# Two layers of attention over 16 images: scores with j on partitions, two heads on halves of the array, a constant softmax shift

## The chip, the cores and the metric

One core of a Trainium2 chip runs the whole program in one launch. The metric is the device time of one execution in microseconds; the median of the runs counts. All data are float32 in HBM at the start and at the end.

## The reference

x has 16 images (b) of 256 channels and 32 x 32 positions. Two layers are applied, each `x = x + attention(groupnorm(x))`:

```
gn: for each image and each pair of neighbouring columns h (16 groups):
    subtract the mean over channels, w and the pair; divide by sqrt(var + 1e-5)
q, k, v = Wq.g + bq, Wk.g + bk, Wv.g + bv          (256 x 256 weights, 1024 positions)
4 heads of d = 64:
    s[i, j]   = q_i . k_j + rel_i . q_j             rel[d, i] = rel_h[d, y] + rel_w[d, w]
    attn[i,:] = softmax over j of s[i, :]
    out[d, i] = sum over j of attn[i, j] * v[d, j]
```

For each image, layer and head the scores are 1024 x 1024.

## The kernel before

A unit is one layer of one image; there are 32, ordered so that layer 0 of the next image alternates with layer 1 of the one before. A unit has 8 blocks: 4 heads times two halves of 512 rows i. x of up to three images stays in SBUF (two tiles of 128 channels side by side) and is updated in place.

For a unit, `norm_slices` sums x over columns on VectorE, averages across partitions by a matmul with a constant matrix (`pm`), and subtracts, squares and scales on GpSimd. `v_slices` makes v with positions on partitions. `kq_slices` makes, for each head, one tile with k on partitions 0-63 and q on 64-127; VectorE then copies q to the upper half of `qrel`, whose lower half holds rel. So one matmul over 128 partitions gives both terms of the scores: [q_i; rel_i] . [k_j; q_j].

`scores` (L232) treats 128 rows i at a time: two matmuls of 128 x 128 weights with 512 columns fill two banks of PSUM (L240), VectorE takes the negative row maximum (L248), ScalarE the exponential with that maximum as bias and the row sum (L251), VectorE the reciprocal (L255) and the scaling of the row (L256). `transposes` (L261) turns the block's four tiles, 128 columns j at a time, by four TensorE transposes into a bank of PSUM (L266), and ScalarE or VectorE copies it to SBUF (L271, L273). `attend` (L278) multiplies with v: the weights are v of two heads (128 columns), and the rows of one head are used (L284). `finish` (L292) adds the result and v's bias to x; attn is normalized already.

The order of each engine's queue is the order in which the code emits the work. The loop at the end emits, for each block and each 128 rows, the scores of the current block, then two transposes and two products of the block before, then one slice of the next unit's norm or projections (from the second block of a unit on). Where two units in a row are of the same layer, `kq_slices` of the second come at once at its start. Loads and stores are issued from SP's queue. PSUM holds two tiles of two banks (scores, projections), two of one bank (transposes, means) and two for the output.

Of the kernel before, what the change touches and what calls it, by code (L numbers as in the profile page):

```python
# [9 lines left out]
F32 = mybir.dt.float32  # L10
AF = mybir.ActivationFunctionType
ALU = mybir.AluOpType
AX = mybir.AxisListType


@with_exitstack
def kernel(
# [17 lines left out]
    P = 128  # L35
    B, C, W, H = x.shape
    N = W * H
    NL = len(layers)
    HEADS = layers[0]["rel_h"].shape[1]
    D = C // HEADS  # L40
    CC = C // P
    NT = N // P
    HALF = 512
    NH = N // HALF
    G = 16
    GT = H // G
    COUNT = C * W * GT
    EPS = 1e-5
    IPB = HALF // P
    BPU = HEADS * NH  # L50
    assert (D, CC, NT, NH, NL) == (64, 2, 8, 2, 2)

    const = ctx.enter_context(tc.tile_pool(name="const", bufs=1))
# [3 lines left out]
    bpool = ctx.enter_context(tc.tile_pool(name="bpool", bufs=6))  # L57
    vpool = ctx.enter_context(tc.tile_pool(name="vpool", bufs=2))
    ppool = ctx.enter_context(tc.tile_pool(name="ppool", bufs=10))
    stat = ctx.enter_context(tc.tile_pool(name="stat", bufs=6))  # L60
    ptpool = ctx.enter_context(tc.tile_pool(name="ptpool", bufs=4))
    ps_s = ctx.enter_context(tc.tile_pool(name="ps_s", bufs=2, space=bass.MemoryType.PSUM))
    ps_t = ctx.enter_context(tc.tile_pool(name="ps_t", bufs=2, space=bass.MemoryType.PSUM))
    ps_o = ctx.enter_context(tc.tile_pool(name="ps_o", bufs=2, space=bass.MemoryType.PSUM))

# [1 line left out]
    xt = {}  # L67

    def load_x(b):
        xt[b] = xpool.tile([P, CC, N], F32, tag="x", name=f"x_{b}")  # L70
        for cc in range(CC):
            nc.sync.dma_start(
                xt[b][:, cc, :], x[b, cc * P : (cc + 1) * P].rearrange("p w h -> p (w h)")
            )

    load_x(0)

# [1 line left out]
    ident = const.tile([P, P], F32, tag="ident", name="ident")  # L79
    make_identity(nc, ident)  # L80
    avg = const.tile([P, P], F32, tag="avg", name="avg")
    nc.vector.memset(avg, 1.0 / COUNT)
    mhalf = const.tile([P, H], F32, tag="mhalf", name="mhalf")
    nc.vector.memset(mhalf, -0.5)

    wkq, wv, bkq, bv, qrel = [], [], [], [], []
    for li, lw in enumerate(layers):
        wkq_l = const.tile([P, CC, HEADS, P], F32, tag=f"wkq{li}", name=f"wkq{li}")
        wv_l = const.tile([P, CC, C], F32, tag=f"wv{li}", name=f"wv{li}")
# [45 lines left out]
    for b in range(1, B):  # L135
        units += [(b, 0), (b - 1, 1)]
# [139 lines left out]
    outs = {}  # L276
# [102 lines left out]
```

## Time and profile before

| | us |
|---|---|
| median of 3 runs | 5371.05 (5367.75, 5371.05, 5399.57) |
| span of the profiled execution | 5370.3 |
| TensorE (PE) busy | 5209.0 |
| VectorE (DVE) busy | 3353.1 |
| ScalarE (ACT) busy | 2041.9 |
| GpSimd (POOL) busy | 589.5 |
| HBM, mean over the span | 7 GB/s |

The time of the profiled execution is known by its span alone, from the first to the last instruction: 5370.3 us, 0.8 us under the median. "PE" rows are matmul instructions, "PEld" rows the loads of their weights, which may overlap matmuls; a matmul's row reaches from its start to its modelled end, so rows in a row overlap. "Idle before" is the time for which the engine had nothing to run ahead of these instructions, with what ended it.

### The profile page before, as it was taken

The numbers are of one execution on the slowest core, as the hardware profiler recorded it, in microseconds if no ns is written. First come the engines' busy times: TensorE is split into PE (matmuls) and PEld (weight loads), VectorE is DVE, ScalarE is ACT, GpSimd is POOL, SyncE is SP. The second block draws the span as 40 slices with busy tenths as digits, with TensorE's granted clock in tenths as the row PEclk, the third lists the DMA queues.
The fourth block names the chain that finished last, engine by engine and source line by source line (L and its number), as shares of the span: only waits on it lengthen the run. The fifth ranks groups of instructions, "written<-read, shape, count | busy, mean of one in ns | idle before, by whom it ended". The sixth has DMA issues, their size and how long they took to land.

```text
span 5370.3 us, 46932 instructions
## 1 busy us (share of the span) xinstructions
PE 5209.0 (97%) x18712; PEld 2788.6 (52%) x18712; DVE 3353.1 (62%) x4694; ACT 2041.9 (38%) x3265; POOL 589.5 (11%) x134
## 2 busy tenths in 40 slices
PE   6999999999999999999999999999999999999999
PEld 3555555555555555555555555555555555555555
DVE  4666666666666666666666666666666666666666
ACT  2333333333333333333333333333333333333333
POOL 2001110011100111101111001110011100111000
PEclk9999999999999999999999999999999999999999
DMA  1000000000000000000000000000000000000000
GB/s 36 1 1 4 12 0 16 1 5 12 0 16 1 5 12 1 16 1 4 12 1 16 0 5 12 0 16 1 5 12 1 16 0 5 12 4 4 1 8 8
DMA packets 13787, 38.28 MB, mean 7 GB/s; under 512 B 3840, under 2 KB 5376, under 8 KB 13568
## 3 DMA queue, kind: packets, MB, share of 16 engines
q1 hardware_dynamic: 13568, 35.27, 1.8%
q8 instruction: 148, 2.42, 0.2%
q14 instruction: 71, 0.58, 0.0%
HBM read 18.49 MB, written 16.78 MB: 7 GB/s over the span
## 4 chain that ended last, share of the span: by engine, by line
PE 88%; POOL 5%; DVE 5%; ACT 1%; issue 0%; DMA 0%; SPq 0%; POOLq 0%
PE po L284 31%; PE ps L240 30%; PE pt L266 15%; PE pk L214 8%; PE pv L198 4%; POOL xc L172 3%; POOL sq L174 2%; DVE nmax L248 2%; ACT p L251 1%; DVE red_v L145 1%; DVE p L256 1%; DVE at L273 0%; PE pm_v L154 0%; DVE rden L255 0%; DMA wn<-in_L_conv_Wk_dram 0%
## 5 line engine op out<-in xcount | busy, mean ns | idle before, releaser
L284 PE MATMUL po<-at,v 128*128 128x512 f32 x4096 | 2116.0, 603 | 120.2 <-DVE at L273 120.0
L240 PE MATMUL ps<-kq,qrel 128*128 128x512 f32 x4096 | 1986.9, 599 | 1.0 <-ACT p L251 0.9
L248 DVE TENSOR_REDUCE nmax<-ps 128x1 f32<-128x1024 f32 x1024 | 1252.2, 1223 | 756.3 <-PE ps L240 754.7
L266 PEld LDWEIGHTS pt<-ident,p 128*128 128x128 f32 x8192 | 1020.9, 142 | 960.4 <-issue 779.6
L271 ACT COPY at<-pt 128x512 f32<-128x512 f32 x1024 | 600.5, 586 | 2277.9 <-PE pt L266 2277.8
L251 ACT ACTIVATE p<-ps,nmax 128x1024 f32<-128x1024 f32 x1024 | 1141.2, 1114 | 349.5 <-DVE nmax L248 349.4
L266 PE MATMUL pt<-ident,p 128*128 128x128 f32 x8192 | 1200.7, 275 | 0.3 <-DVE p L256 0.2
L240 PEld LDWEIGHTS ps<-kq,qrel 128*128 128x128 f32 x4096 | 764.0, 192 | 836.6 <-issue 823.2
L273 DVE COPY at<-pt 128x512 f32<-128x512 f32 x1024 | 705.2, 689 | 377.4 <-PE pt L266 377.3
L284 PEld LDWEIGHTS po<-at,v 128*128 128x128 f32 x4096 | 635.1, 191 | 428.7 <-DVE at L273 314.4
L256 DVE TENSOR_SCALAR p<-p,rden 128x1024 f32<-128x1024 f32 x1024 | 828.8, 809 | 34.8
L172 POOL TENSOR_TENSOR xc<-x,mean 128x2048 f32<-128x2048 f32 x32 | 144.8, 4526 | 4070.5 <-DVE mean L170 4070.5
L214 PE MATMUL pk<-xc,wkq 128*128 128x512 f32 x1024 | 463.6, 592 | 0.0
L225 DVE COPY qrel<-kq 64x1024 f32<-64x1024 f32 x128 | 88.3, 690 | 461.0 <-ACT kq L222 461.0
L214 PEld LDWEIGHTS pk<-xc,wkq 128*128 128x128 f32 x1024 | 192.3, 190 | 230.6 <-issue 216.7
L222 ACT ACTIVATE kq<-pk,bkq 128x1024 f32<-128x1024 f32 x128 | 142.6, 1114 | 445.4 <-PE pk L214 445.4
L255 DVE RECIPROCAL rden<-den 128x1 f32<-128x1 f32 x1024 | 167.0, 163 | 205.6 <-ACT p L251 153.2
L198 PE MATMUL pv<-wv,xc 128*128 128x256 f32 x1024 | 239.5, 383 | 10.7 <-POOL xc L184 10.7
L198 PEld LDWEIGHTS pv<-wv,xc 128*128 128x128 f32 x1024 | 194.2, 192 | 62.9 <-issue 22.2
L183 POOL TENSOR_TENSOR rstd<-var,mhalf 128x32 f32<-128x32 f32 x32 | 173.7, 5429 | 443.0 <-DVE rden L255 277.8
L298 DVE SCALAR_TENSOR_TENSOR x<-po,bv,x 64x512 f32<-64x512 f32 x256 | 191.7, 749 | 41.7 <-PE po L284 41.6
L251 ACT ACTIVATION_READ_ACCUMULATOR p<-ps,nmax 128x1 f32 x1024 | 197.5, 193 | 0.0
(25 smaller groups left out, 602.5 us busy)
## 6 DMA issues: line engine op xcount, KB each, us to landing
x<-in_x_dram SPq DMA_DIRECT2D x32, 512.0 KB, 4.2
out_dram<-x SPq DMA_DIRECT2D x32, 512.0 KB, 2.6
wn<-in_L_conv_Wk_dram SPq DMA_DIRECT2D x2, 256.0 KB, 3.7
wn<-in_L_conv_Wq_dram SPq DMA_DIRECT2D x2, 256.0 KB, 4.2
wn<-in_L_conv_Wv_dram SPq DMA_DIRECT2D x2, 256.0 KB, 4.5
rh<-in_L_conv_rel_h_dram SPq DMA_DIRECT2D x2, 32.0 KB, 3.3
rw<-in_L_conv_rel_w_dram SPq DMA_DIRECT2D x2, 32.0 KB, 2.8
bkq<-in_L_conv_bk_dram SPq DMA_DIRECT2D x2, 1.0 KB, 4.1
```

Source lines behind the costliest of these rows:

```text
L172: nc.gpsimd.tensor_tensor(rows(xc), rows(src), per_column(mean), ALU.subtract)
L198: nc.tensor.matmul(pv[:, i, :], xns[u][:, cc, t * P : (t + 1) * P], wv[l][:, cc, :], start=(cc == 0), stop=(cc == CC - 1),)
L214: nc.tensor.matmul(pk[:, nh, :], wkq[l][:, cc, h, :], xns[u][:, cc, nh * HALF : (nh + 1) * HALF], start=(cc == 0), stop=(cc == CC - 1),)
L240: nc.tensor.matmul(ps[:, nh, :], qrel[l][:, h, i0 : i0 + P], kqs[u, h][:, nh * HALF : (nh + 1) * HALF], start=True, stop=True,)
L248: nc.vector.tensor_reduce(nmax, ps, AX.XY, ALU.max, negate=True)
L251: nc.scalar.activation(p.rearrange("p (a n) -> p a n", a=NH), ps, AF.Exp, bias=nmax, accum_out=den)
L256: nc.vector.tensor_scalar(p, p, rden, None, ALU.mult)
L266: nc.tensor.transpose(pt[:, s * P : (s + 1) * P], probs[blk, s][:, j * P : (j + 1) * P], ident)
L271: nc.scalar.copy(t, pt)
L273: nc.vector.tensor_copy(t, pt)
L284: nc.tensor.matmul(outs[blk], vts[u][:, j, c0 : c0 + P], attnT.pop((blk, j)), start=(j == 0), stop=(j == NT - 1),)
L298: nc.vector.scalar_tensor_tensor(xs, outs.pop(blk)[r0 : r0 + D, :], bv[l][r0 : r0 + D, cc : cc + 1], xs, ALU.add, ALU.add)
```

## The change

The kernel gets two paths. `fast_path` is always run; `general_path`, a loop over images that works much as the old kernel does with a row maximum, follows it behind a branch. It is run if any softmax denominator of the fast path lies outside 1e-22 to 1e24.

In `fast_path` a block is a pair of heads (`pr`) and 512 rows i, 4 blocks a unit, and a step (blk, j) treats 128 positions j, 8 steps a block. k and q of two heads lie in one tile each, head 0 on partitions 0-63 and head 1 on 64-127, so that each score matmul has 64 rows of weights. The scores come with j on partitions and i along the columns. The term with rel is made in two parts: `positions` multiplies q with rel_h and rel_w (64 values for each j instead of 1024), and splits the result in two float32r tiles, `hi` and `lo`; in `scores` these are multiplied with `pick`, a constant matrix of zeros and ones that spreads the 64 values to the columns i. The exponential has the constant 36 subtracted in place of the maximum. Its result is the moving operand of the product with v directly; each head's result goes to its own 64 partitions of one bank. VectorE adds up the eight exponential tiles of a block; a matmul with ones sums them over partitions; the denominators go by DMA from one partition to 64 (8 on each), are inverted there, written to HBM, and read back spread to all partitions; `finish` multiplies with them. `den_all` keeps them for the test at the end.

The loop emits for each step its scores, after each odd step the products with v of two earlier steps, at the fourth step of a block the denominators of the block before and at its last step that block's `finish`, and then a slice of the next unit's preparation (from the unit's second block on). `norm_slices` has five empty slices where it had three, and two after each sum where it had one. PSUM holds three tiles of two banks (scores, projections, sums) and two for the output. The weights are loaded ahead of x, by `load_weights`, with 14 transfers a layer. `project` is as before, with two heads' k (or q) in one product; `values` is as before.

```diff
+def fast_path(ctx, tc, sh, x, out, W, den_all):
...
+    LAG = 2
...
+    ppool = ctx.enter_context(tc.tile_pool(name="ppool", bufs=8))
...
+    ps_s = ctx.enter_context(tc.tile_pool(name="ps_s", bufs=3, space=bass.MemoryType.PSUM))
+    ps_o = ctx.enter_context(tc.tile_pool(name="ps_o", bufs=2, space=bass.MemoryType.PSUM))
...
+    def positions(u, pr):
+
+        l = units[u][1]
+        pa = psum2(f"pa_{u}_{pr}")
+        for nh in range(NH):
+            nc.tensor.matmul(
+                pa[:, nh, :],
+                W.rel[l][:, pr, :],
+                qs[u, pr][:, nh * HALF : (nh + 1) * HALF],
+                start=True,
+                stop=True,
+            )
+        hi = kqpool.tile([P, N], F32R, tag="hi", name=f"hi_{u}_{pr}")
+        lo = kqpool.tile([P, N], F32R, tag="lo", name=f"lo_{u}_{pr}")
+        nc.scalar.copy(hi.rearrange("p (a n) -> p a n", a=NH), pa)
+        nc.vector.tensor_tensor(
+            lo.rearrange("p (a n) -> p a n", a=NH),
+            pa,
+            hi.bitcast(F32).rearrange("p (a n) -> p a n", a=NH),
+            ALU.subtract,
+        )
+        abh[u, pr], abl[u, pr] = hi, lo
...
+    def scores(blk, j):
+        u, pr, half = blk
+        ps = psum2(f"ps_{u}_{pr}_{half}_{j}")
+        jc = slice(j * P, (j + 1) * P)
+        ic = slice(half * HALF, (half + 1) * HALF)
+        hs = [slice(0, D), slice(D, P)]
+        for h in range(2):
+            nc.tensor.matmul(
+                ps[:, h, :], ks[u, pr][hs[h], jc], qs[u, pr][hs[h], ic], start=True, stop=False
+            )
+        for part, last in ((abh, False), (abl, True)):
+            for h in range(2):
+                nc.tensor.matmul(
+                    ps[:, h, :], part[u, pr][hs[h], jc], W.pick[hs[h], ic], start=False, stop=last
+                )
+        p = ppool.tile([P, 2, HALF], F32, tag="p", name=f"p_{u}_{pr}_{half}_{j}")
+        nc.scalar.activation(p, ps, AF.Exp, bias=W.shift)
+        probs[blk, j] = p
+        if j == 1:
+            accs[blk] = apool.tile([P, 2, HALF], F32, tag="acc", name=f"acc_{u}_{pr}_{half}")
+            nc.vector.tensor_tensor(accs[blk], probs[blk, 0], p, ALU.add)
+        elif j > 1:
+            nc.vector.tensor_tensor(accs[blk], accs[blk], p, ALU.add)
+
+    def attend(blk, j):
+        u, pr, half = blk
+        if j == 0:
+            outs[blk] = ps_o.tile([P, HALF], F32, tag="o", name=f"po_{u}_{pr}_{half}")
+        p = probs.pop((blk, j))
+        for h in range(2):
+            c0 = pr * P + h * D
+            nc.tensor.matmul(
+                outs[blk][h * D : (h + 1) * D, :],
+                vts[u][:, j, c0 : c0 + D],
+                p[:, h, :],
+                start=(j == 0),
+                stop=(j == NT - 1),
+            )
...
+    def denominators(blk):
...
+        pd = psum2(f"pd_{name}")
+        acc = accs.pop(blk)
+        for h in range(2):
+            nc.tensor.matmul(
+                pd[h * D : (h + 1) * D, 0, :], W.ones[:, :D], acc[:, h, :], start=True, stop=True
+            )
+        den = fpool.tile([P, HALF], F32, tag="den", name=f"den_{name}")
+        nc.scalar.copy(den, pd[:, 0, :])
+        for h in range(2):
+            nc.sync.dma_start(den_all[h * D : (h + 1) * D, n, :], den[h * D : h * D + 1, :])
+        r8 = fpool.tile([P, 8], F32, tag="r8", name=f"r8_{name}")
+        nc.vector.reciprocal(r8, den_all[:, n, :])
+        rd = dpool.tile([2, HALF], F32, tag="rd", name=f"rd_{name}")
+        nc.sync.dma_start(rd.rearrange("h (a b) -> (h a) b", b=8), r8)
+        rden = fpool.tile([P, HALF], F32, tag="rden", name=f"rden_{name}")
+        nc.sync.dma_start(rden, rd.unsqueeze(1).to_broadcast([2, D, HALF]))
+        return rden
...
+    def finish(blk):
...
+        nc.vector.tensor_tensor(o, outs.pop(blk), rdens.pop(blk), ALU.mult)
+        nc.vector.scalar_tensor_tensor(xs, o, W.bv[l][:, pr : pr + 1], xs, ALU.add, ALU.add)
...
+    for g in range(len(steps) + LAG):
+        if g < len(steps):
+            scores(*steps[g])
+        if g % 2 == 1:
+            for a in (g - LAG - 1, g - LAG):
+                if 0 <= a < len(steps):
+                    attend(*steps[a])
+
+        n, c = divmod(g, NT)
+        if c == LAG + 1 and n > 0:
+            rdens[blocks[n - 1]] = denominators(blocks[n - 1])
+        if c == NT - 1 and n > 0:
+            finish(blocks[n - 1])
...
+                if u + 1 < len(units):
+                    prep = chain(norm_slices(u + 1), projection_slices(u + 1))
+            next(prep, None)
...
+    fast_path(tc, sh, x, out, W, den_all)
...
+        nc.vector.tensor_scalar(low, flatden, DEN_LO, None, ALU.is_ge)
...
+        nc.vector.scalar_tensor_tensor(good, flatden, DEN_HI, low, ALU.is_le, ALU.mult)
...
+    ok = nc.values_load(flag[0:1, 0:1], min_val=0, max_val=P)
+    with tc.If(ok < P):
+        general_path(tc, sh, x, layers, out, W)
```

## Rows read from the trace of the kernel before

**Rows 1.** The page's head, busy time by engine, and the granted TensorE clock.

```profile
span 5370.3 us, 46932 instructions
PE 5209.0 (97%) x18712; PEld 2788.6 (52%) x18712; DVE 3353.1 (62%) x4694; ACT 2041.9 (38%) x3265; POOL 589.5 (11%) x134
PEclk9999999999999999999999999999999999999999
```

**Rows 2.** The page's chain that ended last, by engine and line.

```profile
PE po L284 31%; PE ps L240 30%; PE pt L266 15%; PE pk L214 8%; PE pv L198 4%; POOL xc L172 3%; POOL sq L174 2%; DVE nmax L248 2%; ACT p L251 1%; DVE red_v L145 1%; DVE p L256 1%; DVE at L273 0%; PE pm_v L154 0%; DVE rden L255 0%; DMA wn<-in_L_conv_Wk_dram 0%
```

**Rows 3.** Groups by form, TensorE matmuls: count, busy us, mean ns, idle before.

```profile
L284 PE MATMUL po<-at,v 128*128 128x512 f32 x4096 | 2116.0, 603 | 120.2 <-DVE at L273 120.0 <-ACT at L271 0.2
L240 PE MATMUL ps<-kq,qrel 128*128 128x512 f32 x4096 | 1986.9, 599 | 1.0 <-ACT p L251 0.9
...
L266 PE MATMUL pt<-ident,p 128*128 128x128 f32 x8192 | 1200.7, 275 | 0.3 <-DVE p L256 0.2
...
L214 PE MATMUL pk<-xc,wkq 128*128 128x512 f32 x1024 | 463.6, 592 | 0.0
L198 PE MATMUL pv<-wv,xc 128*128 128x256 f32 x1024 | 239.5, 383 | 10.7 <-POOL xc L184 10.7
...
L154 PE MATMUL pm_v<-red_v,avg 128*128 128x16 f32 x128 | 17.1, 246 | 12.0 <-DVE red_v L145 12.0
```

**Rows 4.** The chain in order of time, projections: start us, us, what.

```profile
214.51 13.73 PE pk L214 x32
```

**Rows 5.** Timeline, TensorE, two stretches: start, us, engine, line, operation, idle before.

```profile
2000.64 1.88 PE L240 MATMUL ps<-kq,qrel 128*128 128x512 f32 x4
2000.65 0.19 PEld L240 LDWEIGHTS ps<-kq,qrel 128*128 128x128 f32 x1 [0.24 <-issue]
...
2001.08 0.19 PEld L240 LDWEIGHTS ps<-kq,qrel 128*128 128x128 f32 x1 [0.24 <-issue]
...
2002.36 0.60 PE L266 MATMUL pt<-ident,p 128*128 128x128 f32 x4
...
5356.07 0.30 PEld L284 LDWEIGHTS po<-at,v 128*128 128x128 f32 x2 [0.48 <-ACT at L271]
```

**Rows 6.** Groups by form, ScalarE and VectorE.

```profile
L251 ACT ACTIVATE p<-ps,nmax 128x1024 f32<-128x1024 f32 x1024 | 1141.2, 1114 | 349.5 <-DVE nmax L248 349.4
...
L271 ACT COPY at<-pt 128x512 f32<-128x512 f32 x1024 | 600.5, 586 | 2277.9 <-PE pt L266 2277.8
...
L298 DVE SCALAR_TENSOR_TENSOR x<-po,bv,x 64x512 f32<-64x512 f32 x256 | 191.7, 749 | 41.7 <-PE po L284 41.6
...
L255 DVE RECIPROCAL rden<-den 128x1 f32<-128x1 f32 x1024 | 167.0, 163 | 205.6 <-ACT p L251 153.2
...
L222 ACT ACTIVATE kq<-pk,bkq 128x1024 f32<-128x1024 f32 x128 | 142.6, 1114 | 445.4 <-PE pk L214 445.4
...
L145 DVE TENSOR_REDUCE red_v<-sq 128x16 f32<-128x1024 f32 x64 | 77.7, 1215 | 116.5 <-POOL sq L174 116.5
...
L205 ACT COPY v<-pv 128x1024 f32<-128x1024 f32 x64 | 64.8, 1012 | 248.1 <-PE pv L198 248.1
...
L119 DVE TENSOR_TENSOR qrel<-rh,rw 64x1024 f32<-64x1024 f32 x8 | 9.5, 1221 | 0.1
```

**Rows 7.** Groups by form, GpSimd.

```profile
L183 POOL TENSOR_TENSOR rstd<-var,mhalf 128x32 f32<-128x32 f32 x32 | 173.7, 5429 | 443.0 <-DVE rden L255 277.8 <-DVE var L179 165.2
L172 POOL TENSOR_TENSOR xc<-x,mean 128x2048 f32<-128x2048 f32 x32 | 144.8, 4526 | 4070.5 <-DVE mean L170 4070.5
```

**Rows 8.** DMA issues by line: count, KB each, median us from issue to landing.

```profile
bkq<-in_L_conv_bk_dram SPq DMA_DIRECT2D x2, 1.0 KB, 4.1
```

**Rows 9.** Timeline of the start: one issue of SP's queue, the first scores.

```profile
5.22 0.60 SPq L115 DMA_DIRECT2D rh<-in_L_conv_rel_h_dram x1
...
68.07 3.60 PE L240 MATMUL ps<-kq,qrel 128*128 128x512 f32 x8
```

More of the change, by code (lines that the diff above doesn't have):

```diff
@@ L182, in norm_slices, with project @@
         rstd = small.tile([P, H], F32, tag="rstd", name=f"rstd_{u}")
-        nc.gpsimd.tensor_tensor(rstd, var, mhalf, ALU.pow)
-        nc.gpsimd.tensor_tensor(rows(xc), rows(xc), per_column(rstd), ALU.mult)
+        nc.gpsimd.tensor_tensor(rstd, var, W.mhalf, ALU.pow)
+        nc.gpsimd.tensor_tensor(rows(xc, H), rows(xc, H), per_column(rstd), ALU.mult)
         xns[u] = xc
-        for _ in range(3):
+        for _ in range(5):
             yield
-    def v_slices(u):
+    def project(u, pr, which):
@@ L230 @@
-    probs = {}
-    def scores(blk, s):
-        u, h, half = blk
-        l = units[u][1]
-        i0 = half * HALF + s * P
-        name = f"{u}_{h}_{half}_{s}"
-        ps = ps_s.tile([P, NH, HALF], F32, tag="s", name=f"ps_{name}")
+        w, bias = (W.wk, W.bk) if which == "k" else (W.wq, W.bq)
+        pk = psum2(f"p{which}_{u}_{pr}")
+        for nh in range(NH):
+            for cc in range(CC):
+                nc.tensor.matmul(
+                    pk[:, nh, :],
+                    w[l][:, cc, pr * P : (pr + 1) * P],
+                    xns[u][:, cc, nh * HALF : (nh + 1) * HALF],
+                    start=(cc == 0),
+                    stop=(cc == CC - 1),
+                )
@@ L256, in scores @@
-        nc.vector.tensor_scalar(p, p, rden, None, ALU.mult)
-        probs[blk, s] = p
-    attnT = {}
-    def transposes(blk, j):
-        u, h, half = blk
-        pt = ps_t.tile([P, HALF], F32, tag="t", name=f"pt_{u}_{h}_{half}_{j}")
-        for s in range(IPB):
-            nc.tensor.transpose(
-                pt[:, s * P : (s + 1) * P], probs[blk, s][:, j * P : (j + 1) * P], ident
-            )
-        t = ptpool.tile([P, HALF], F32, tag="at", name=f"at_{u}_{h}_{half}_{j}")
-        if j % 2 == 0:
-            nc.scalar.copy(t, pt)
-        else:
-            nc.vector.tensor_copy(t, pt)
-        attnT[blk, j] = t
@@ L292, in finish @@
+    rdens = {}
     def finish(blk):
[L294 removed]
+        u, pr, half = blk
         b, l = units[u]
[L296 to L306 removed]
@@ L309 @@
-    for f in (norm_slices, v_slices, kq_slices):
+        xs = xt[b][:, pr, half * HALF : (half + 1) * HALF]
+        o = fpool.tile([P, HALF], F32, tag="o", name=f"o_{u}_{pr}_{half}")
+        nc.vector.tensor_tensor(o, outs.pop(blk), rdens.pop(blk), ALU.mult)
+        nc.vector.scalar_tensor_tensor(xs, o, W.bv[l][:, pr : pr + 1], xs, ALU.add, ALU.add)
+        if l == NL - 1 and half == NH - 1:
+            nc.sync.dma_start(flat(out[b, pr * P : (pr + 1) * P]), xt[b][:, pr, :])
+    for f in (norm_slices, projection_slices):
@@ new lines, in fast_path @@
+    for n, blk in enumerate(blocks):
+        index[blk] = n
+    steps = [(blk, j) for blk in blocks for j in range(NT)]
+    BPU = CC * NH * NT
+    prep = iter(())
+    for g in range(len(steps) + LAG):
[10 more added lines that the diff above has]
+            finish(blocks[n - 1])
+        u, step = divmod(g, BPU)
+        if g < len(steps):
+            if step == NT:
```

536 lines of the change are left out of this document (344 added, 192 removed).

## The prediction

> **What bounds the kernel now.** I read the page's busy shares first: TensorE is busy for 5209.0 of 5370.3 us at an almost full clock [rows 1]; the other engines are not near it. The chain of waits agrees: by line it is the products with v (31%), the scores (30%) and the transposes (15%) [rows 2]. Then the groups by form, to see what TensorE does: the scores are 2048 matmuls in the code but 4096 MATMUL rows, so a float32 matmul is two instructions, while a transpose is one (8192 rows) [rows 3]. Last the order of time, for the rate. Sixteen projection matmuls, 32 instructions, take 13.73 us [rows 4]: **t = 0.429 us** from start to start of a 512-column instruction. The mean of 0.6 us in [rows 3] is longer because instructions overlap. The timeline shows t between weight loads too (2000.65, 2001.08), and each load starts where the matmul before it starts, so it is hidden under it [rows 5]. Four 128-column transposes end after 0.60 us, the last of them 0.275 long [rows 3, 5], so they start 0.108 apart, a quarter of t: time goes by the columns streamed, and nothing shows a gain from using half of the array's rows or columns.
>
> So the change is worth what it takes off TensorE's stream. Each of 256 blocks (a head, half of the rows) has 16 score instructions, 32 transposes and 16 instructions with v: 16t + 8t + 16t = 17.2 us, 4393 us in all; the projections and norms add 737 [rows 3].
>
> **The change, part by part.** It has 128 blocks of 8 steps, 1024 steps. One step gives two heads' scores for 128 columns j and 512 rows i.
>
> Scores: two float32 matmuls (4 instructions of t) and four in float32r. No row shows float32r. Bounds: t, since a float32 instruction of as many columns takes that, and t/2, since a float32 matmul takes 2t for a product of two split operands (four part products), of which one remains. I take t/2, the part-product row being the nearest; t stays for the range.
>
> The two heads lie on rows 0-63 and 64-127 of the array. Whether two such matmuls run side by side is the question; no row shows it. From above: no overlap, 4t + 2t = 6t a step. From below: full overlap, 3t. I take overlap in program order, since rows show instructions of one stream starting strictly one after another [rows 5]: an instruction starts when the one before it has started and its own half is free. The code issues both instructions of head 0, then both of head 1, so head 0's first runs alone (0 to t), its second beside head 1's first (t to 2t), head 1's second beside head 0's first float32r; the last float32r ends at 4t and the next step begins at 3.5t. Two steps take **7.5t**, against 12t alone.
>
> Products with v: issued for two steps at once after odd steps, heads on column halves. Four instructions a step; by the same reckoning 2t a step plus t once: **5t** for two steps, against 8t alone. The transposes and their copies out of PSUM are gone.
>
> Change of layout: row halves, column halves and the whole array follow each other. A break in the stream is seen only where a wait ends: the second of two loads, each 0.19 long, ends 0.30 after the first starts, so loads stand 0.11 apart [rows 5], and a matmul outlasts the next start by 0.6 - 0.43 = 0.17 [rows 3, 4]. So 0.17 + 0.11 = **0.28 us** per change; bounds 0 (nothing shows that a break is needed) and 0.17 + 0.19, a load's whole length. There are two changes per two steps, 32 a unit, and some 15 more where slices of the next unit's preparation come between: 47 x 32 = 1504. The Trainium skill (TensorEngine Tiling (Array Packing), Key Properties) says that a change of tiling mode, not of the tile alone, drains TensorE; no run here shows it, and by it the price of 0 falls away.
>
> Loop: 512 x (12.5 x 0.429 + 2 x 0.28) = 512 x 5.92 = 3032. Denominators: two matmuls with ones per block, behind products in the same layout: 128 x 2t = 110. Projections and means have the same instruction counts as before: 464 + 240 + 34 (twice pm_v's 17.1) = 737 [rows 3]; positions adds 128 matmuls, 256t = 110. Further changes of layout: 15 x 32 x 0.28 = 134. Start: the first scores came at 68.07 [rows 9]; x's load now stands behind 28 weight transfers at some 0.6 us of issue each, and positions adds 3.4, so 75. End: the last denominators, three transfers, out, the check and the branch, some 25. The first unit's preparation is in both the start and the 847, so minus 26. **Sum: 3032 + 110 + 847 + 134 + 74 = 4197, about 4200 us**, 1170 below the span; the span stands 0.8 us under the median of 5371.05, so the same against either.
>
> What lies beside it. ScalarE: 1024 exp and 128 q, k copies at 1.114, 64 copies of v and 64 of positions at 1.01, 128 denominators at 0.59 [rows 6]: 1490 us, hidden. VectorE: the row maxima, the scaling and half of the copies go; 896 additions of 128x1024 at 1.22 (the only two-operand row of that length), 64 subtractions at about as much, 256 operations of block ends at 0.75, 128 reductions at 1.21, 128 reciprocals at 0.16 [rows 6]: 1540 us, hidden. New is the wait in front of each reciprocal: a transfer, 4.1 us for the 1 KB one [rows 8], behind the copy (0.59) and the matmuls (0.86). Behind it on VectorE stand the additions, positions' subtraction and the norm's reductions; TensorE would feel it through the ring of 8 p tiles, of which 4 are in use, so after some four steps of 4.1 us. If that cover were gone it would cost 128 x 5.6 = 710. On SP the write and the broadcast read wait for it and for each other, some 10 us; x's loads and out's stores queue behind, wanted a unit (130 us) later. GpSimd's sweeps stay (at most 4.5 each, pow 5.4 [rows 7]): two of them, or pow and one, 10 us, against five steps (20 us) that the code leaves for each. The 120 us in which TensorE waited for VectorE's copies of transposes [rows 3] go with those copies, and nothing is late next as long as the covers named hold. The general path is code that is jumped over: nothing, but for its test.
>
> **A page against the trace.** In [rows 5] the weight load at 2000.65 runs under the matmul that began at 2000.64, on the same rows of the array. So I hide the column halves' loads, which gives the 4200. The Trainium skill (TensorE: Matmul & The Clock Gate, The mechanism) says that loads overlap matmuls in flight only where the row group differs, and column halves share theirs; by that rule it would be the 4700 of the second rival. This trace disagrees for the whole array (a load 0.01 us behind its matmul's start), and for halves no row shows it.
>
> **The rivals.**
> Slower: the halves do not run side by side. Place: every score and every product with v, 20t for two steps; price 512 x 3.2 = 1648, denominators 110 more: **5955**; with layout changes for nothing, 5530. It decides from the point where less than a third of the expected overlap is had, (5955 - 5370) / (5955 - 4200). For it: time goes by columns alone in every row. Against: the halves read other partitions and write other banks or partitions, and loads already run beside matmuls.
> Loads of the column halves in the open: 4096 instructions with v and 512 of denominators each show a load of 0.108, 498 us: **4700** (5075 with 0.19). [Rows 5] speak against it.
> Row halves alone overlap: 15.5t, denominators 4t: **4970**. Column halves alone: 17t: **5190**.
> Full pairs: 10t for two steps, denominators t: **3595**. Against it is the order in the code, two instructions of one head in a row.
> The denominators' round trip decides: 0.86 + 0.59 + 4.1 + 0.16 + 4.1 + 4.1 + 0.75 = 14.7 us, against 33 us until the PSUM tile is wanted again. It decides from some 10 us per transfer; with 12 each, 128 x 5.4 = 690 more: **4890**.
> The change doesn't do what it says: a denominator outside the bounds runs the general path behind it, at least another kernel's worth, over 9000. By the reference q and k spread by 0.8 (weights 0.05, 256 channels), the scores by about 10 (64 products of q with k and with a sum of two unit normals), so row maxima lie some 15 to 50; the bounds admit -14 to 91.
>
> **How the numbers follow.** The forecast with its unknown prices runs from 3780 (free layout changes) to 4650 (float32r at t, 1.5t x 512 = 329 more; layout at 0.36, 120 more). Chances: forecast 0.60; loads shown 0.06; rows only 0.08; columns only 0.03; full pairs 0.05; round trip 0.02; no overlap 0.14; general path 0.02. The range 3590 to 4970 leaves out columns only, no overlap and the general path, 0.19. The runs differ by 0.6%, so 1% is about what a measurement can tell from no change. Faster is 0.84 by the cases, slower 0.16; of no overlap, a case with a little of it could fall within 1%: 0.83, 0.02, 0.15.
>
> **What would show it.** Side by side: two score rows of different heads that start within t of each other; the time from a step's first score instruction to the next step's is 1.5 us (2.57 without). A product with v: 0.86 per step. Layout: idle TensorE of 0.28 between groups. Float32r: 0.21 from start to start. VectorE busy for 1540 us, ScalarE for 1490; reciprocals waiting 4 to 6 us for a transfer with no idle TensorE behind them. The prediction is wrong if steps take over 5 us, or if TensorE waits for exp, a PSUM tile or a transfer.

## The result, and the profile after

The changed kernel takes 3866.36 us (median of 4 runs, 3860.08 to 3871.47), the kernel before 5384.53 in the same comparison: a ratio of 0.718 (95% interval 0.716 to 0.721). The forecast was 4200 in a range of 3590 to 4970. The time lies inside it, 334 us below the forecast, but the runs below show that this distance is the remainder of two errors of opposite sign: the loop is shorter than forecast by 616 us, and stalls that were costed at nothing, with the half clock behind them, give back some 360.

The head of the changed kernel's page, its clock line and the two lines of its chain answer to [rows 1, 2]:

```profile
span 3861.6 us, 37025 instructions
PE 3538.8 (92%) x15386; PEld 1501.0 (39%) x15386; DVE 1705.3 (44%) x1556; ACT 1490.2 (39%) x1409; POOL 676.1 (18%) x134
PEclk9999999999999999999999999999999999999998
PE 53%; POOL 16%; DMA 16%; DVE 12%; issue 2%; SPq 1%; ACT 1%; DVEq 0%; POOLq 0%
PE ps L233 12%; DMA rden<-rd 12%; PE po L257 11%; PE pq L152 7%; PE pv L196 6%; PE pk L152 6%; PE ps L238 5%; POOL xc L128 4%; POOL rstd L139 4%; DVE acc L248 4%; POOL xc L140 4%; POOL sq L130 4%; PE pa L170 3%; DMA rd<-r 3%; DMA den_all<-den 2%; PE pd L276 2%
```

TensorE is still the engine that bounds the kernel, but it is busy for 92% of the span where it was for 97% [rows 1], and it holds only 53% of the chain, where its lines added up to 88% [rows 2]: a DMA (rden<-rd, 12%) has entered it, and GpSimd's share has grown from 5% [rows 2] to 16%. The digits of the clock line hide a change too. The mean granted clock went from 0.992 to 0.963; if the clock stands at either 1 or 0.5 of full speed, that is 2 x 0.037 x 3861.6 = 286 us at half clock, against 86 before. Such a figure is rough: the four runs of the changed kernel have clocks from 0.956 to 0.963, worth 27 us of time by this reckoning, while their times lie within 12 us and do not follow the clock. The clock terms in the accounts below are that uncertain, and so a sum that meets its measurement within a few us does so in part by luck.

The timeline of TensorE shows two steps of the loop, from one score instruction at 2005.44 to the same one two steps later (columns: start us, us, engine, line, operation, count):

```profile
2005.44 1.13 PE L233 MATMUL ps<-q,k 64*128 64x512 f32 x4
2006.00 0.80 PE L238 MATMUL ps<-pick,hi 64*128 64x512 f32 x2
2006.63 0.41 PE L238 MATMUL ps<-pick,lo 64*128 64x512 f32 x2
2006.86 1.03 PE L233 MATMUL ps<-q,k 64*128 64x512 f32 x4
...
2008.29 1.94 PE L257 MATMUL po<-p,v 128*64 128x512 f32 x8
2008.77 0.14 PEld L257 LDWEIGHTS po<-p,v 128*64 128x64 f32 x2 [0.28 <-issue]
2009.20 0.14 PEld L257 LDWEIGHTS po<-p,v 128*64 128x64 f32 x2 [0.28 <-issue]
2010.16 1.13 PE L233 MATMUL ps<-q,k 64*128 64x512 f32 x4
```

Two steps take 4.72 us; the forecast had 5.92. The eight product instructions take 1.94, that is four starts of t = 0.429 and a tail: they run two by two, and a pair's two weight loads stand in one row (2008.77, 2009.20, 0.43 apart), under matmuls that are running. The four float32 score instructions run from 2006.86 and the float32r ones follow: with 0.23 from `lo` to the next start (2006.63, 2006.86), one step's scores in the stream are 2 x 0.429 + 2 x 0.23 = 1.32 us.

The groups by form answer to [rows 3, 6, 7] (columns: count, busy us, mean ns, idle us before them and what ended it):

```profile
L248 DVE TENSOR_TENSOR acc<-acc,p 128x1024 f32<-128x1024 f32 x768 | 1121.0, 1460 | 603.5 <-ACT p L242 574.2 <-DVE acc L248 0.9
L257 PE MATMUL po<-p,v 128*64 128x512 f32 x4096 | 1036.2, 628 | 123.1 <-DVE o L298 123.1
...
L152 PE MATMUL pq<-xc,Wq 128*128 128x512 f32 x512 | 271.7, 680 | 108.0 <-POOL xc L140 108.0
...
L298 DVE TENSOR_TENSOR o<-po,rden 128x512 f32<-128x512 f32 x128 | 88.6, 692 | 701.4 <-DMA rden<-rd 656.0 <-PE ps L238 45.4
```

Here are the stalls. TensorE waits 123.1 us for VectorE's `o`, which empties the PSUM tile that the products write, and 108.0 us for GpSimd's `xc`, of which 10.7 belong to the start. With 39.5 us in front of the denominators' matmuls (`pd`) that is 260 us inside the loop. VectorE's `o` itself waits 656.0 us for the transfer of the reciprocals. Pow takes 6.4 us and the additions 1.46 on average, against 5.43 [rows 7] for pow and 1.22 [rows 6] for an addition of that length before.

The chain in order of time, once through a place where both stalls occur (start us, us, what):

```profile
2009.12 1.21 DVE red_v L104
2010.33 2.25 DVE red_m L104 x2
2012.58 0.12 DVE r L284
...
2012.72 2.03 DMA rd<-r
...
2014.77 6.96 DMA rden<-rd
...
2021.75 0.70 DVE o L298
...
2026.83 0.11 DVE var L135
...
2027.01 6.45 POOL rstd L139
...
2033.52 4.66 POOL xc L140
...
2038.23 5.40 PE pq L152 x8
```

The reciprocal `r` stands behind four reductions of the norm on VectorE, two of squares (red_v) and two of x (red_m). The code emits it ahead of all four: `r` at step 11 of a unit's 32 (counted from 0), the sums of the squares at step 15, and these sums of x only in the next unit (their mean is taken at 2116.49). So VectorE does not work in the order in which the code emits the work, which the section on the kernel before gives for every engine. What this place costs shows beside the block before, whose reciprocal has no reduction ahead of it (timeline: start us, us, engine, line, operation, idle before):

```profile
1979.29 1.03 PE L276 MATMUL pd<-acc,ones 128*64 128x512 f32 x4
1983.40 0.20 DVE L284 RECIPROCAL r<-den_all 128x8 f32<-128x8 f32 x1 [3.03 <-DMA den_all<-den]
1992.59 0.69 DVE L298 TENSOR_TENSOR o<-po,rden 128x512 f32<-128x512 f32 x1 [6.54 <-PE ps L238]
...
1999.76 1.03 PE L276 MATMUL pd<-acc,ones 128*64 128x512 f32 x4
...
2007.98 2.35 DVE L104 TENSOR_REDUCE red_v<-sq 128x16 f32<-128x1024 f32 x2 [3.49 <-POOL sq L130]
```

From the denominators' matmuls to `r` it is 4.11 us in the block before and 12.82 here, where VectorE stands 3.49 us for GpSimd's squares and then reduces; from `r` to `o` it is 9.19 and 9.17, in this block a write of 2.03 us and a broadcast read of 6.96. Over the units of the trace the first is 12.8 us on average in this block and 4.2 to 4.6 in the other three of a unit, the second 8.9 to 9.1 in all four. The products of the next block but one need the PSUM tile that `o` reads. TensorE comes to them at 2018.34, 18.6 us after the denominators' matmuls, and waits 4.15 us. Behind `o` and some additions comes `var`, then pow (6.45) and the scaling (4.66) on GpSimd, and the projections of the next unit start only at 2038.23.

The stretches between, by engine (stretch us; then PE, PEld, DVE, ACT, POOL busy us with counts, granted clock, DMA share, GB/s):

```profile
2005.00:2018.00 13.00, 13.00 (x72) 5.90 (x68) 7.03 (x7) 5.40 (x5) 2.95 (x1) 1.00 0.03 9
2018.30:2022.40 4.10, 0.05 (x2) 0.00 (x0) 0.65 (x1) 1.11 (x1) 0.00 (x0) 0.95 0.10 37
2022.50:2025.40 2.90, 2.90 (x8) 0.77 (x8) 2.80 (x3) 0.00 (x0) 0.00 (x0) 0.50 0.00 0
2034.00:2038.20 4.20, 0.31 (x4) 0.00 (x0) 0.00 (x0) 1.11 (x1) 4.17 (x1) 1.00 0.13 46
2039.20:2042.40 3.20, 3.20 (x5) 1.35 (x4) 1.98 (x3) 0.00 (x0) 0.00 (x0) 0.50 0.01 5
```

TensorE is busy for 0.05 of the 4.10 us before 2022.4 and for 0.31 of the 4.20 before 2038.2. After each of the two idle stretches the granted clock is 0.50, the level of 1.2 GHz, for about 3 us of work. A stall of 4 us therefore costs some 1.5 us more than itself, half of the 3 us.

### The profile page after: what moved, and what is told of

Read it like the earlier page. It is cut to its first block, busy times and chain, and to the rows that moved or that the text cites. A ratio compares the mean times of both kernels' runs of the same rounds, so it can differ in the third digit from the quotient of the medians.

```text
span 3861.6 us, 37025 instructions
## 1 busy us (share of the span) xinstructions
PE 3538.8 (92%) x15386; PEld 1501.0 (39%) x15386; DVE 1705.3 (44%) x1556; ACT 1490.2 (39%) x1409; POOL 676.1 (18%) x134
## 4 chain that ended last, share of the span: by engine, by line
PE 53%; POOL 16%; DMA 16%; DVE 12%; issue 2%; SPq 1%; ACT 1%; DVEq 0%; POOLq 0%
PE ps L233 12%; DMA rden<-rd 12%; PE po L257 11%; PE pq L152 7%; PE pv L196 6%; PE pk L152 6%; PE ps L238 5%; POOL xc L128 4%; POOL rstd L139 4%; DVE acc L248 4%; POOL xc L140 4%; POOL sq L130 4%; PE pa L170 3%; DMA rd<-r 3%; DMA den_all<-den 2%; PE pd L276 2%
## 5 line engine op out<-in xcount | busy, mean ns | idle before, releaser
L242 ACT ACTIVATE p<-ps,shift 128x1024 f32<-128x1024 f32 x1024 | 1141.4, 1115 | 1006.3 <-PE ps L238 996.4
L248 DVE TENSOR_TENSOR acc<-acc,p 128x1024 f32<-128x1024 f32 x768 | 1121.0, 1460 | 603.5 <-ACT p L242 574.2
L257 PE MATMUL po<-p,v 128*64 128x512 f32 x4096 | 1036.2, 628 | 123.1 <-DVE o L298 123.1
L233 PE MATMUL ps<-q,k 64*128 64x512 f32 x4096 | 1132.2, 629 | 0.0
L238 PE MATMUL ps<-pick,hi 64*128 64x512 f32 x2048 | 826.4, 800 | 0.0
L233 PEld LDWEIGHTS ps<-q,k 64*128 64x128 f32 x4096 | 341.9, 187 | 493.4 <-issue 335.1
L257 PEld LDWEIGHTS po<-p,v 128*64 128x64 f32 x4096 | 255.4, 139 | 622.5 <-issue 479.2
L238 PE MATMUL ps<-pick,lo 64*128 64x512 f32 x2048 | 411.0, 393 | 0.0
L298 DVE TENSOR_TENSOR o<-po,rden 128x512 f32<-128x512 f32 x128 | 88.6, 692 | 701.4 <-DMA rden<-rd 656.0
L152 PE MATMUL pq<-xc,Wq 128*128 128x512 f32 x512 | 271.7, 680 | 108.0 <-POOL xc L140 108.0
L196 PE MATMUL pv<-Wv,xc 128*128 128x256 f32 x1024 | 237.8, 385 | 0.0
```

Of the source, the lines that this page charges most:

```text
L152: nc.tensor.matmul(pk[:, nh, :], w[l][:, cc, pr * P : (pr + 1) * P], xns[u][:, cc, nh * HALF : (nh + 1) * HALF], start=(cc == 0), stop=(cc ...
L196: nc.tensor.matmul(pv[:, i, :], xns[u][:, cc, t * P : (t + 1) * P], W.wv[l][:, cc, :], start=(cc == 0), stop=(cc == CC - 1),)
L233: nc.tensor.matmul(ps[:, h, :], ks[u, pr][hs[h], jc], qs[u, pr][hs[h], ic], start=True, stop=False)
L238: nc.tensor.matmul(ps[:, h, :], part[u, pr][hs[h], jc], W.pick[hs[h], ic], start=False, stop=last)
L242: nc.scalar.activation(p, ps, AF.Exp, bias=W.shift)
L248: nc.vector.tensor_tensor(accs[blk], accs[blk], p, ALU.add)
```

## Experiments

Theory A: halves of the array run in full pairs, whatever the order in the code, in rows and in columns; what is lost beside that is the two stalls of a unit and the half clock after them. Rivals were that only one of the two kinds of halves pairs, that pairing hangs on the order in which the code issues the heads, and that the stalls are not separate but one chain. All ratios are against the kernel before, and all changes are counted from the changed kernel's 3866 unless another run is named.

**Row halves taken away.** k is kept per head, padded with zeros to 128 rows, so a score has the whole array and the halves of rows are gone; the products keep their column halves. The norm's and q's buffers are one fewer to make room.

```
-                ps[:, h, :], ks[u, pr][hs[h], jc], qs[u, pr][hs[h], ic], start=True, stop=False
+                ps[:, h, :], ks[u, pr][h][:, jc], qs[u, pr][:, ic], start=True, stop=False
-                    ps[:, h, :], part[u, pr][hs[h], jc], W.pick[hs[h], ic], start=False, stop=last
+                    ps[:, h, :], part[u, pr][:, jc], W.pickz[h][:, ic], start=False, stop=last
```

> The scores on all 128 rows of the array: k of each head padded with zeros, pick too; two buffers fewer in two pools to make room; same result. Theory A, the row halves run side by side in full: a step's scores go from the 1.32 us of the changed kernel to 4 x 0.429 + 4 x 0.229 = 2.63, 1340 us more, less the stalls of 265 us and their half clock, which longer steps hide: 4800 to 5200. Theory B, most of the change's gain comes from the transposes and VectorE's work that went, and the row halves bring little: under 4100.

Measured: 4742.83 us, ratio 0.882 (0.880 to 0.884), just under the range. The timeline of its TensorE has one step's scores:

```profile
2003.76 1.98 PE L250 MATMUL ps<-q,kz 128*128 128x512 f32 x4
2005.18 1.02 PE L255 MATMUL ps<-pickz,hi 128*128 128x512 f32 x2
2006.04 0.62 PE L255 MATMUL ps<-pickz,lo 128*128 128x512 f32 x2
```

Four float32 instructions now stand alone one after another (from 2003.76 to the 1.98 of their row) and the float32r ones take twice as long as a pair did: 2.63 us a step for 1.32, 1341 us over 1024 steps. That is the size that full pairing of the rows asks for. The time grew by 877 only, for three reasons that I can count: the stalls (260) went into the slack of longer steps, the clock rose to 0.997 (half of 286 - 28 is 129), and the projections' whole array and the scores' are now one layout, so 15 changes of layout a unit fall away (15 x 32 x 0.18 = 86, if these changes cost what those between row and column halves do; no run measures them). 1341 - 260 - 129 - 86 = 866. By this account the range was too high because the last of these was left out.

**The order of the heads.** Each step's scores are issued head by head: the float32 matmul and the two float32r ones of head 0, then the three of head 1. A matmul's partner on the other half now stands three matmuls (four instructions) behind it.

```
-        for part, last in ((abh, False), (abl, True)):
-            for h in range(2):
+            for part, last in ((abh, False), (abl, True)):
```

(The loop over the parts now stands inside the loop over the heads, behind the float32 matmul of the head.)

> The three score matmuls of head 0, then the three of head 1, nothing else changed. Theory P, matmuls start in program order, a float32 matmul as one entry of two passes, each as soon as its half is free: head 1 cannot start before head 0's last has started (2t + 0.229), so a step's period is 4.53t + 0.229 = 2.17 us in place of 1.32; 870 us more, less stalls of up to 370: 4370 to 4740. Theory Q, each half has a queue of its own and order counts for nothing: 3830 to 3900. The prediction's theory, instructions in order with the two passes as two entries, would give the changed kernel 1.5 us a step, and this one more.

Measured: 3867.61 us, ratio 0.719: the same. TensorE's timeline of this kernel:

```profile
2007.10 1.14 PE L233 MATMUL ps<-q,k 64*128 64x512 f32 x4
...
2008.53 1.02 PE L233 MATMUL ps<-q,k 64*128 64x512 f32 x3
2008.98 0.80 PE L237 MATMUL ps<-pick,hi 64*128 64x512 f32 x1
2009.07 0.59 PE L233 MATMUL ps<-q,k 64*128 64x512 f32 x1
```

A step's float32 instructions still stand together, four from 2007.10 and three from 2008.53, although `hi` and `lo` of head 0 come before head 1's in the program: head 1's first float32 instruction starts ahead of two matmuls that were issued before it. One `hi` starts at 2008.98, before the other head's last float32 instruction at 2009.07, so the halves even run a little out of step. This also shows that the new order reached TensorE: in the changed kernel both `hi` (2007.32) start behind all four float32 instructions of their step. Each half takes its own instructions as if it had its own queue, at least as far ahead as this code needs, which is three matmuls. The prediction's rule that an instruction starts only when the one before it in the program has started is refuted. The Trainium skill (TensorE: Matmul & The Clock Gate, The mechanism) likewise says that matmuls start and end strictly in the order of the program; the measurement here differs, and it decides.

**Column halves taken away.** v is laid out with 64 zero columns between the heads of a pair, so that each product has the whole array and both heads add into one bank.

```
-                outs[blk][h * D : (h + 1) * D, :],
-                vts[u][:, j, c0 : c0 + D],
+                outs[blk],
+                vts[u][:, j, pr, h : h + 2].rearrange("p h d -> p (h d)"),
-                start=(j == 0),
-                stop=(j == NT - 1),
+                start=(j == 0 and h == 0),
+                stop=(j == NT - 1 and h == 1),
```

> The products with v on all 128 columns: v of one head beside 64 columns of zeros, both heads added up in the same bank; one buffer fewer in the norm's pool; same result. Theory A, the column halves run side by side in full: two steps' products go from 4t to 8t, 1.72 x 512 = 880 us more, less stalls of up to 370: 4370 to 4750. Theory B, they bring little: under 4000.

Measured: 4383.25 us, ratio 0.815, in the range of A. Its TensorE:

```profile
2004.29 3.70 PE L263 MATMUL po<-p,vz 128*128 128x512 f32 x8
2007.92 1.13 PE L240 MATMUL ps<-q,k 64*128 64x512 f32 x4
```

Eight products take 3.70 us instead of 1.94, from the first start to the next scores 3.63 instead of 1.87: 512 x 1.76 = 901 us. The stalls (260) are again gone in the slack, the clock is 0.998 (half of 286 - 18 is 134): 901 - 260 - 134 = 507, and 517 were measured.

**The reciprocal without its round trip.** VectorE divides into all 128 rows at once; the two transfers are gone, but a reciprocal of 128 x 512 takes their place.

```
-        r8 = fpool.tile([P, 8], F32, tag="r8", name=f"r8_{name}")
-        nc.vector.reciprocal(r8, den_all[:, n, :])
-        rd = dpool.tile([2, HALF], F32, tag="rd", name=f"rd_{name}")
-        nc.sync.dma_start(rd.rearrange("h (a b) -> (h a) b", b=8), r8)
-        nc.sync.dma_start(rden, rd.unsqueeze(1).to_broadcast([2, D, HALF]))
+        nc.vector.reciprocal(rden, den)
```

> The reciprocal is taken of the 128 x 512 denominators in place; the write to HBM and the broadcast read are gone, the DMAs to den_all stay for the test alone. Theory C, both stalls of TensorE in a unit (for VectorE's finish, 123 us, and for GpSimd's scaling, 97 us without the start) and the pd waits (35) come from VectorE's queue standing behind the rden transfer, and each brings a stretch at half clock (285 us of those): 3460 to 3600. Theory D, the prediction's: the cover hides the transfers, and the stalls come from VectorE sharing with GpSimd: 3800 to 3900. A reciprocal of 512 values is some 2.9 us by (201 - 163) / 7 ns for a value; if VectorE becomes late by that, D's number holds too, with other waits.

Measured: 3716.24 us, ratio 0.691 (0.690 to 0.692), between the two theories' ranges and in neither. Its group by form on VectorE:

```profile
L284 DVE RECIPROCAL rden<-den 128x512 f32<-128x512 f32 x128 | 428.4, 3347 | 65.8 <-ACT den L280 65.8
```

And what TensorE waited for (engine, line, whom; us, times, longest):

```profile
PE pq L152 <- POOL xc L140: 130.8, 32, 10.7
```

The wait for `o` is gone from the list, so the denominators' trip was its cause. The edit takes two things out of that trip: the two transfers, and a part of the wait on VectorE, where now one of the four reductions stands ahead of the reciprocal (red_v at 2055.61, the reciprocal at 2056.74, the other three from 2061.67 on). Which of the two was enough is not shown; by the rows above the trip with its transfers fits its slack in the three blocks of a unit where no reduction stands ahead, so the place in the queue alone may have been. The wait for `xc` has not gone with it but grown from 108 to 130.8: it is not just the echo of the first. The account: -123 for `o`, +23 for `xc`, +11 for `pd` (50.3 us), and the clock at 0.979 (half of 286 - 156, -65) make -154; -150 was measured.

**Two more steps for GpSimd.** The code leaves five steps between the scaling of a unit and its first projection; now it leaves seven.

```
-        for _ in range(5):
+        for _ in range(7):
```

(The second of the two loops of this form in `norm_slices`, behind `xns[u] = xc`.)

> Seven empty slices in place of five between GpSimd's scaling and the first projection, nothing else; the write and read of the denominators stay. Theory C2: the wait for GpSimd's scaling (97 us without the start) is a matter of slack alone, steps without preparation being 2.4 us long and not the 4.1 of the prediction, so two steps more (some 5 us) take it away, with 27 stretches at half clock: 3710 to 3760. Rival: VectorE, held up by the transfer, is late with whatever comes next, and the wait moves on: 3830 to 3870.

Measured: 3739.98 us, ratio 0.696, in the range of 3710 to 3760. TensorE's waits in this kernel:

```profile
PE po L257 <- DVE o L298: 119.9, 31, 6.0
...
PE pq L152 <- POOL xc L140: 10.7, 1, 10.7
```

Of the wait for `xc` only the 10.7 us of the start are left, and the wait for `o` stays (119.9 for 123.1). The two stalls are separate, with two remedies.

**Both together.** The edits of the two preceding kernels in one.

> Both: the reciprocal in place and seven empty slices. From 3716: the wait for GpSimd's scaling (120 us without the start) and the half clock behind it (some 45) go: 3540 to 3600, and the granted clock rises above 0.99. Rival as in the run before: 3680 to 3720.

Measured: 3548.15 us, ratio 0.660 (0.659 to 0.661), in the range; 318 us less than the changed kernel. The page's busy times, and its waits:

```profile
PE 3437.4 (97%) x15386; PEld 1479.9 (42%) x15386; DVE 2244.8 (63%) x1556; ACT 1490.2 (42%) x1409; POOL 643.7 (18%) x134
```

```profile
PE pd L276 <- DVE var L135: 50.2, 28, 1.8
PE pq L152 <- POOL xc L140: 10.7, 1, 10.7
```

TensorE is back at 97%, its clock at 0.995, and the loop's remaining wait is 50 us. This is the time that the new loop has without its two stalls: they and the half clock behind them cost the change 318 us.

**Fours instead of twos.** On top of the last kernel the products are issued for four steps at a time, which halves the changes of layout.

```
-        if g % 2 == 1:
-            for a in (g - LAG - 1, g - LAG):
+        if g % 4 == 3:
+            for a in range(g - LAG - 3, g - LAG + 1):
```

> As the run before, with the products with v issued for four steps at once, after every fourth step: half as many changes between row halves and column halves. By the trace of the changed kernel a pair of changes costs 0.37 us, so 256 pairs less are 94 us less than the run before: 3440 to 3500. By the prediction's price (0.28 each) 143 less. Rival: no change in price, or the products come too late for the PSUM tile or the p tiles: the run before or more.

Measured: 3634.63 us, ratio 0.676: a miss, 86 us more than with twos, which is the rival's side. Its longest wait:

```profile
PE ps L233 <- DVE var L135: 145.5, 31, 4.9
```

Four steps of scores without products between them take 5.3 us, and in that time the PSUM tile that holds the variance's sum (`pm_v`) is still unread: on VectorE `o`, the addition to x, a reduction and four additions of exponentials stand ahead of `var`, which comes 6.8 us behind `pm_v` (2012.40 to 2019.19). TensorE waits 31 times 4.7 us, and the clock falls to 0.973. Against the kernel with twos: +145 of this wait, -50 of `pd`, +80 of clock, -92 of layout: +83 for 86 measured.

**Denominators two steps later**, on top of the fours, so that VectorE has them out of its way.

```
-        if c == LAG + 1 and n > 0:
+        if c == LAG + 3 and n > 0:
```

> As the run before, with the denominators' matmuls two steps later, when VectorE's additions are done. If the waits of these matmuls for VectorE (50 us with the reciprocal in place) are the last ones left, 40 to 60 us less than the run before. Rival: the multiplication with the reciprocal then comes too late for the next block's PSUM tile, more than the run before.

Measured: 3650.28 us, ratio 0.679: 16 us more, no gain. The expectation's condition did not hold, since the run before has no wait for `pd` any more. The wait for `var` is 133.6 us, hardly less, and the clock 0.966. TensorE does not wait for `o` either, so the rival's reason was not at work; what makes the 16 us is open.

**Six and six.** The steps are spread differently: six for GpSimd's subtraction and squares, six for pow and scaling (five and seven in the kernel with both edits), on top of the local reciprocal and still with twos.

```
-        for _ in range(5):
+        for _ in range(6):
```

(Both loops of this form.)

> The reciprocal in place, with six empty slices before the second sum and six before the projections, in place of five and seven; products in twos. VectorE then no longer stands for 3.5 us in each unit waiting for GpSimd's squares (113 us in the changed kernel), so the denominators' waits for it (50 us) go: 3490 to 3520. Rival: these waits come from VectorE's work itself (the additions beside GpSimd's sweeps): 3540 to 3560, as with five and seven.

Measured: 3536.21 us, ratio 0.658 (0.657 to 0.659): 12 us or 0.3% less than five and seven, which the two intervals hardly tell apart, and not the 30 to 60 expected. VectorE's wait for the squares is 8.3 us in this kernel and was 8.3 already with five and seven (113.1 in the changed kernel), so there was nothing left of it to take away. TensorE still waits 44.4 us for `pd`, 6 us less than before (50.2), and the rival was the better account.

**Six and six with fours.**

> The same slices with the products in fours. In fours alone TensorE stood 145 us behind a PSUM tile that VectorE had not read yet (the sum's, for var). If VectorE's stand for the squares made it late, the stall goes and fewer changes of layout count: 90 us less than the run with twos, 3400 to 3440. Rival: VectorE's queue itself is too full at that point (reciprocal 3.35, additions, reductions): 3550 to 3640.

Measured: 3444.11 us, ratio 0.641 (0.640 to 0.642), the best of all kernels here; 4 us above the range of 3400 to 3440. The page's busy times, the timeline of TensorE over four steps, and its wait in the loop:

```profile
PE 3356.0 (97%) x15386; PEld 1520.0 (44%) x15386; DVE 2127.3 (62%) x1556; ACT 1489.6 (43%) x1409; POOL 674.3 (20%) x134
```

```profile
2003.10 1.13 PE L233 MATMUL ps<-q,k 64*128 64x512 f32 x4
...
2008.60 3.65 PE L257 MATMUL po<-p,v 128*64 128x512 f32 x16
2012.18 1.13 PE L233 MATMUL ps<-q,k 64*128 64x512 f32 x4
```

```profile
PE pd L276 <- DVE var L135: 31.2, 28, 1.1
```

Four steps take 9.08 us; twice the two steps of the changed kernel is 9.44. The two changes of layout that are saved are 0.36 us together, 0.18 each, 92 us over 256 groups of four. The time fell by 92 us against twos at six and six, where 13 us less of `pd` should have made it 105, so about 13 us of this account stay unexplained. (The clock has no part in it: 0.998 in three of the four runs of either kernel.) The scores' wait for `var` of the fours at five and seven does not occur, but not for the reason expected. VectorE stands for the squares as long as there (116.5 us in both kernels), and `var` comes 6.6 us behind `pm_v` (2016.36 to 2022.95) where it was 6.8. What changed is the place of `pm_v`: one step later, so that one step of scores and then the 3.65 us of products follow it, where two steps of scores did, the second of which needed the tile. That the range was nearly met was luck in this point.

## Why the prediction was right or wrong

**The sum.** In the prediction's terms the loop was forecast at 512 x 5.92 = 3032 us and measured at 512 x 4.72 = 2417. Of the 616 less, 294 are the scores (7.5t = 3.22 forecast, 2.64 measured), 220 the products (5t, measured 4t), 102 the changes of layout (0.28, measured 0.18). The further changes of layout are 48 less by the same price, and the first scores came at 71.8 (75 forecast). Against it stand 260 us of stalls and half of the 200 us by which the stretches at half clock grew. 4197 - 616 - 51 + 260 + 100 = 3890, 28 above the span of 3861.6.

That the time lies in the range is luck. By its own signs the prediction was wrong, since TensorE waits for a PSUM tile that a transfer holds up. Without the two stalls that it denied the time is the 3548 us of the run with both edits, below the range.

**The step that failed first** is the rule "an instruction starts when the one before it has started and its own half is free". Nothing in [rows 5] showed two instructions that could have run together, so the rule was an extension of rows on the whole array to halves. The order of the heads changes nothing (3867.6 for 3866.4), and halves run out of step in that kernel: the halves pair in full. That is the rival of full pairs. With its loop (10t, layout at 0.28) and without stalls the rival gave 3595, to which the slip in its denominators adds 55 (two starts of t a block, as in the forecast, and not one): 3650. The stall-free kernel measured 3548. The evidence against it, the code's order, did not carry.

**The step that failed second** is the covers. The reciprocal's wait was said to be hidden by the ring of p tiles. It was not the ring but the PSUM tile that ran out. The trip itself was sized well: where nothing stands ahead of the reciprocal it took 13.3 us (1979.29 to 1992.59) for the 14.7 of the rival, although its parts differ (6.96 for the broadcast read, where each transfer was put at the 4.1 of a 1 KB row [rows 8]). Two other terms were wrong. The 33 us of slack were worked out at 4.1 us a step; at the measured 2.36 eight steps are 18.9, and 18.6 were there. And the norm's reductions were placed behind the reciprocal on VectorE; once a unit they stand ahead of it and make the trip 22.0 us. So it outlasted its slack on one block a unit, and only there: 31 times 4 us. The second stall has the first of these roots too. GpSimd's five steps were taken as 20 us at the mean step of 4.1. The norm's slices fall on the steps without projections, of 2.36 us, so five are 11.8 us; pow and scaling measure 6.4 + 4.7 = 11.1 and `var` itself comes late. A slack counted in steps had to be priced with the steps of its own stretch. Both stalls were then removed one by one and together (-150, -126, -318).

**What the stalls cost beyond themselves** was no term of the forecast at all: 286 us at half clock in the rows, 28 and 18 in the kernels with longer steps and 35 in the one without stalls.

**Steps that held.** ScalarE at 1490 us (1490.2). Float32r at t/2 = 0.214: 0.23 us lie between `lo` and the next start (2006.63, 2006.86). The other terms, start and end, projections, denominators: 4197 - 616 - 51 = 3530 with the loop as measured. The span of the kernel without the two stalls is 3543, but 50 us of waits for `pd` and some 18 of clock are in it, so these terms together were too high by some 55 us (28 by the sum above). The loads of the column halves cost nothing: the rival of 4700 would show 4096 loads in the open, and the rows at 2008.77 and 2009.20 lie within the 1.94 us of the matmuls. The Trainium skill (TensorE: Matmul & The Clock Gate, The mechanism) states that loads overlap matmuls in flight only where the row group differs, beside a sentence that also lets loads into the background weight buffer go ahead; in this trace loads of column halves on the same rows overlap, and the measurement decides. The price of a change between row and column halves is 0.18 us, under the 0.28 taken, and not nothing: the Trainium skill (TensorEngine Tiling (Array Packing), Key Properties) says that a change of mode drains the engine, and the fours agree with that.

**Sizes that were off** without consequence for the sign: VectorE is busy for 1705 us and not 1540. Its additions beside GpSimd's sweeps take up to 5.6 us each (1.22 forecast), and the mean of 1.46 stands in front of `o` and `var` in the same queue. The general path did not run, and the copies of transposes took their 120 us of waits with them.

**What stays open.** The 13 us in the account of the best kernel; the 16 us of the later denominators; whether the first stall would go if the reciprocal kept its transfers and stood ahead of the reductions on VectorE, which no run tries; what a change between the whole array and a half costs; and how far ahead a half can look in the queue, of which only three matmuls are shown.

## What to carry to other kernels

Packing two small heads on halves of the array halves TensorE's time for both kinds of halves; the order in which the partners are issued needed no care here, but every change between row and column halves cost 0.18 us, so group what has the same layout. When the bounding engine becomes faster, convert every slack that is counted in steps to the new steps' length, stage by stage, before calling another engine hidden, and read each engine's order in the trace: VectorE's was not the code's, and that decided which block stalled. The remaining stall costs more than its length when the clock falls behind it. A wait is settled only by removing it alone and beside the others: two stalls that looked like one chain in the trace had two causes.

## What the runs showed of the hardware that was not expected

- Matmuls on halves of the array run in full pairs, whatever their order in the program within three matmuls (3867.6 us and 3866.4).
- A broadcast read that fills 256 KB on 128 partitions from DRAM took 6.96 us in the chain, where a 1 KB transfer took 4.1 [rows 8].
- After a stretch in which TensorE stood idle for 4.10 us the granted clock was 0.50 in the next 2.90 us of work, and again after 4.20 us with 0.31 of work.
- A reciprocal of 128 x 512 takes 3.35 us on VectorE, five times its multiplication of that size (0.69), and is still the better choice against two transfers.
- VectorE's additions took 1.46 us on average and up to 5.6 beside GpSimd's sweeps, 1.22 alone.
